# Six instead of eight experts with places of their own in a routed expert stage

## The chip, the cores and the metric

The kernel runs on one core of a Trainium2 chip, in one launch. The metric is device time in microseconds, the median over several executions. A profile of one further execution gives the engines' instructions (PE is TensorE, DVE VectorE, ACT ScalarE, POOL GpSimd, SP SyncE) and the packets of the DMA engines. All data are float32.

## The reference

One layer of a perceiver block on 256 tokens of width 512: attention to 4096 context tokens and to the tokens themselves, then a state-space mixer, then a mixture of experts. The change concerns only the last part. With x the normalized tokens:

```python
scores = sigmoid(x @ gate_w)                       # 256 x 32 experts
topk_w, topk_i = top_k(scores, 6)
topk_w = topk_w / (sum(topk_w) + 1e-20)
combine = sum(one_hot(topk_i, 32) * topk_w)        # 256 x 32
g = einsum('td,edf->tef', x, wg); u = einsum('td,edf->tef', x, wu)    # 192 wide for each expert
routed = einsum('tef,efd,te->td', silu(g) * u, wd, combine)
shared = (silu(x @ sg) * (x @ su)) @ sd
out = x_before + routed + shared
```

Every token uses 6 of 32 experts, so 1536 pairs of token and expert are computed rather than 8192. How many tokens an expert gets depends on the data. Counted with the reference on the inputs that it sets up, experts 0 to 7 get 19, 65, 18, 38, 100, 75, 55 and 21; the ten largest of the rest get 63 to 103, and the other fourteen 1 to 43.

## The kernel before

The kernel is one program written by hand in its order; a scheduler then settles how the instructions of each engine follow one another, and adds the waits. Attention and the mixer fill the span to about 800 us; the routing follows to 838 us, and the expert rounds from there to the end.

**Routing.** route(t) (lines 1003 to 1023) computes the gate for 128 tokens and picks six experts each. scatter(t) (1025) writes each token's row, six times, into a DRAM buffer xg, in which every expert has 256 rows. places() (1041) counts the tokens of every expert and ranks those experts that have no place of their own by their count; place_rows() (1099) turns the ranking into row numbers, one column of the table `place` for each transfer that has to find its expert through the table.

**Places.** The 32 experts are handled at 32 places, two at a time, in 16 rounds of a pair each. The first FIXED places belong to the experts of those numbers. The next ten are wide and go to the largest of the remaining experts. All places up to WIDE hold up to 128 tokens; the others are narrow and hold 64, so that both experts of a narrow pair share one tile of 128 tokens. If an expert has more tokens than its place, a flag (`crowded`, 1128) sends the program into a second arm (1574 to 1597), which redoes all pairs for two tiles of tokens each.

```python
FIXED = 8                                              # 57
WIDE = FIXED + 10                                      # 58
NPL = 2 * (NE - FIXED) + (NE - WIDE) // 2 - (NE - WIDE) + (NE - FIXED) // 2   # 62: columns of place
ZROW = WIDE * P + (NE - WIDE - TAIL) * HALFP           # 63: rows of the result buffer ye
```

**Weights.** A pair's weights are two pieces of 1 MB (gate, up and the first 128 rows of the down matrix, 8 KB for each of 128 partitions) and one of 256 KB (the rest of the down matrix). There are NHELD = 6 sets of buffers. load_weights (1173) loads a pair:

```python
if fixed:                                              # 1175
    for i in range(2):
        wait_for(nc.sync.dma_start(to[i], a["experts"][2 * n + i]), behind)
    nc.sync.dma_start(to[2], a["down_rest"][2 * n:2 * n + 2].rearrange("e p n -> (e p) n"))
else:
    s = 2 * n - FIXED                                  # 1180
    for i in range(2):
        rows_at(to[i], a["experts"].rearrange("e p n -> (e p) n"), s + i)
    rows_at(to[2], a["down_rest"].rearrange("e p n -> (e p) n"), NE - FIXED + s // 2)
```

A pair of fixed places is known beforehand: SP loads it by plain DMA (L1177, L1178) from hold() (1191), as soon as the mixer has finished with two large buffers. The others are found through the table: POOL issues an indirect DMA for each piece (rows_at, L1165) once place_rows has written the table: pairs 4 and 5 in the loop at 1306, and pair n + 5 in round n (load_pair, 1552), behind the down product that frees its buffers.

**Rounds.** The loop at 1524 runs over the pairs n. A wide round does gate_up (1430: two products of 128 tokens, written by project at L218, with silu on ACT and a product on DVE), fetches the tokens of pair n + 2 (fetch, 1353: SP and plain DMA, L1359, for a pair of fixed places, POOL and an indirect DMA otherwise), transposes the tokens of pair n + 1 (turn, L1369), computes the down product of pair n - 1 (down, L1458 and L1461) with two copies by ACT and two result writes to ye, and transposes its own hidden values (L1448). A narrow round has one token tile for both experts: gate_up_halves (L1388) runs two products on halves of the array, down_halves (L1410, L1411) gives one result tile and one write. The token tiles live in a ring of four buffers. The pairs 0 and 1 take their tokens by a product with a selection matrix (L1474) instead, and the last four pairs add their results on chip by another one (spread, L1428), rather than through ye. At the end POOL gathers the results of the other pairs from ye for each token (L1321), DVE adds them (L1329), and SP stores the output.

Of the kernel before, what the change touches and what calls it, by code (L numbers as in the profile page):

```python
# [53 lines left out]
WGU = KD * 2 * FE  # L54
WEX = WGU + DM
NHELD = 6
FIXED = 8
WIDE = FIXED + 10
HALFP = P // 2
HEAD = 4  # L60
TAIL = 8
NPL = 2 * (NE - FIXED) + (NE - WIDE) // 2 - (NE - WIDE) + (NE - FIXED) // 2
ZROW = WIDE * P + (NE - WIDE - TAIL) * HALFP
# [10 lines left out]
def perceiver_layer(ctx: ExitStack, tc: tile.TileContext, a: dict, out: bass.AP):  # L74
# [65 lines left out]
    def layer(ctx, bounded):  # L140
# [848 lines left out]
        def routing_memory():  # L989
# [8 lines left out]
            G.iota(m["p"], pattern=[[0, 1]], base=0, channel_multiplier=1, allow_small_or_imprecise_dtypes=True)  # L998
            V.tensor_scalar(m["free"], m["p"], float(FIXED), None, ALU.is_ge)

# [40 lines left out]
        def places():  # L1041


            mask, first, pos, key, keys, at, less = (m[n] for n in ("mask", "first", "pos", "key", "keys", "at", "less"))
            few, n, low = slice(0, NE), NE - FIXED, slice(FIXED, NE)

# [21 lines left out]

            wide = float(WIDE - FIXED)
            V.tensor_scalar(first[:, low], at[:, low], float(P), float(FIXED * P), ALU.mult, ALU.add)  # L1070
            V.tensor_scalar(less[:, low], at[:, low], wide, 0.0, ALU.subtract, ALU.max)
# [580 lines left out]
```

## Time and profile before

| | |
|---|---|
| median of 3 executions | 985.41 us (983.65 to 986.29) |
| the profiled execution | 989.13 us |
| its span, from first to last instruction | 987.4 us |
| granted TensorE clock | 0.998 |
| PE busy | 964.3 us, 98% |
| DVE, ACT, POOL busy | 496.5, 388.1, 205.0 us |
| moved by DMA | 125.65 MB, 41.16 MB of it on the software queue (POOL's) |

A line of instructions in the profile gives the source line, the engine, the operation and "out<-in" by the names of the tiles. A tile that reuses the memory of an older one carries the older one's name: the weight pieces appear as w_in, wkv, ctx, w_out, oacc, kT and lacc, the last piece as v or oacc. The releaser in brackets is what the profile infers to have ended an idle time. Times inside the span count from its start.

### The profile page before, as it was taken

To read this page: it belongs to the slowest core of one execution; us is meant where nothing else is said; L and a number is where in the kernel's file an instruction comes from. 1 tells how busy PE (TensorE), PEld (TensorE's weight loads), DVE (VectorE), ACT (ScalarE), POOL (GpSimd) and SP (SyncE) were. 2 spreads that over 40 slices of the span, in tenths; PEclk is the share of its full clock that TensorE was granted. 3 is DMA by queue.
4 is the path that set the end of the run, shared out by engine and by line. 5 is a ranking of instruction groups with operands and counts; after the bars stand their busy time and mean duration, and the time that the engine had idled before them with its cause. 6 is when DMAs were issued, how large, how long until landed. Compare 5 with 4: busy or idle time off the path is not lost.

```text
span 987.4 us, 8877 instructions
## 1 busy us (share of the span) xinstructions
PE 964.3 (98%) x2730; PEld 453.8 (46%) x2730; DVE 496.5 (50%) x1000; ACT 388.1 (39%) x854; POOL 205.0 (21%) x212
## 2 busy tenths in 40 slices
PE   7999999999999999999999999999999999999995
PEld 3444444444444444444444444444465655455442
DVE  3456554454454544544545445458587666521133
ACT  3645443443444434434434344344153731122220
POOL 4443001101100200200200110000013234545442
PEclk9999999999999999999999999999999999999999
DMA  9733232213304304304113121250046452899973
GB/s 317 237 74 98 76 95 91 71 32 117 85 11 139 85 1 149 75 11 150 53 33 97 67 51 32 72 152 1 0 150 206 171 188 111 319 342 352 381 292 107
DMA packets 131436, 125.65 MB, mean 127 GB/s; under 512 B 80209, under 2 KB 99570, under 8 KB 126130
## 3 DMA queue, kind: packets, MB, share of 16 engines
q1 hardware_dynamic: 119216, 77.96, 26.1%
q0 software_dynamic: 7984, 41.16, 11.4%
q10 hardware_dynamic: 4178, 5.85, 1.6%
q8 instruction: 24, 0.39, 0.2%
q14 instruction: 34, 0.28, 0.1%
HBM read 89.02 MB, written 35.93 MB: 127 GB/s over the span
## 4 chain that ended last, share of the span: by engine, by line
PE 94%; DVE 2%; ACT 1%; POOL 1%; issue 1%; DMA 1%; SPq 0%; DVEq 0%; ACTq 0%
PE oT L592 23%; PE scT L567 23%; PE ps_kv L364 17%; PE ps_egu L218 5%; PE ps_self L218 3%; PE ps_v L218 2%; PE ps_o L790 2%; PE ps_egu L1388 2%; PE ps_k L218 2%; PE ps_ye L1458 2%; PE ps_xbc L218 1%; PE ps_out L984 1%; PE ps_sgu L218 1%; PE xgTp L1369 1%; PE ps_ye L1461 1%; PE ps_yd L924 1%
## 5 line engine op out<-in xcount | busy, mean ns | idle before, releaser
L583 DVE TENSOR_TENSOR lacc<-lacc,prT 128x512 f32<-128x512 f32 x256 | 182.8, 715 | 238.9 <-ACT prT L573 238.2
L573 ACT ACTIVATE prT<-scT,bq,rk 128x512 f32<-128x512 f32 x256 | 198.9, 777 | 253.8 <-PE scT L567 241.7
L567 PE MATMUL scT<-qT,kT 128*128 128x512 f32 x536 | 271.6, 592 | 0.0
L592 PE MATMUL oT<-prT,v 128*128 128x512 f32 x528 | 268.3, 592 | 0.0
L567 PEld LDWEIGHTS scT<-qT,kT 128*128 128x128 f32 x536 | 101.1, 190 | 124.7 <-issue 122.4
L592 PEld LDWEIGHTS oT<-prT,v 128*128 128x128 f32 x528 | 100.2, 190 | 125.8 <-issue 115.5
L196 POOL TENSOR_TENSOR rk<-pv,mhalf 128x4 f32<-128x4 f32 x32 | 32.3, 1010 | 369.2 <-DVE pv L195 369.2
L364 PE MATMUL ps_kv<-wkv,fast 128*128 128x512 f32 x112 | 53.4, 592 | 0.0
L254 ACT ACTIVATE sq<-kraw 128x128 f32<-128x128 f32 x128 | 35.6, 278 | 45.3 <-DVE kraw L382 43.2
L364 PE MATMUL ps_kv<-wkv,ctx 128*128 128x512 f32 x112 | 52.8, 592 | 0.0
L364 PE MATMUL ps_kv<-fast,fast 128*128 128x512 f32 x112 | 52.6, 592 | 0.0
L598 DVE TENSOR_TENSOR oacc<-oT,oacc 128x512 f32<-128x512 f32 x64 | 43.7, 683 | 0.0
L364 PEld LDWEIGHTS ps_kv<-wkv,fast 128*128 128x128 f32 x112 | 21.3, 190 | 26.8 <-issue 26.8
L364 PEld LDWEIGHTS ps_kv<-fast,fast 128*128 128x128 f32 x112 | 21.3, 190 | 26.8 <-issue 21.8
L364 PEld LDWEIGHTS ps_kv<-wkv,ctx 128*128 128x128 f32 x112 | 21.3, 190 | 26.8 <-issue 23.7
L358 POOL TENSOR_TENSOR fast<-ctx 128x512 f32<-128x512 f32 x7 | 9.3, 1335 | 113.0 <-PE ps_kv L364 94.2
L382 DVE TENSOR_TENSOR kraw<-ps_kv,fast 128x256 f32<-128x256 f32 x42 | 17.9, 426 | 28.1 <-PE ps_kv L364 28.1
L1441 DVE TENSOR_TENSOR hid<-si,ps_egu 128x128 f32<-128x128 f32 x18 | 5.2, 287 | 51.7 <-ACT si L1439 49.0
L790 PE MATMUL ps_o<-wo,qT 128*128 128x512 f32 x64 | 28.8, 592 | 0.0
L218 PE MATMUL ps_self<-wq,xT 128*128 128x512 f32 x64 | 28.1, 592 | 0.0
L603 DVE RECIPROCAL lacc<-ps_l 128x512 f32<-128x512 f32 x8 | 26.8, 3349 | 0.1
L364 PE MATMUL ps_kv<-fast,ctx 128*128 128x512 f32 x56 | 26.3, 592 | 0.0
(379 smaller groups left out, 1120.8 us busy)
## 6 DMA issues: line engine op xcount, KB each, us to landing
xg<-xn SPq DMA_DIRECT2D x6, 2560.0 KB
ctx<-in_ctxT_dram SPq DMA_DIRECT2D x7, 1024.0 KB, 5.3
kd<-tr SPq DMA_DIRECT2D x112, 64.0 KB, 2.7
kT<-kd SPq DMA_DIRECT2D x28, 256.0 KB, 3.7
ye<-y_sb ACTq DMA_DIRECT2D x21, 256.0 KB, 7.9
wq<-in_wq_dram SPq DMA_DIRECT2D x4, 1024.0 KB
wo<-in_wo_dram SPq DMA_DIRECT2D x4, 1024.0 KB
w_in<-in_W_inT_dram SPq DMA_DIRECT2D x4, 1024.0 KB
```

The costliest lines, as they stand in the source:

```text
L196: return G.tensor_tensor(dst, v[:, :n], mhalf[:, :n], ALU.pow)
L218: TE.matmul(ps, lhs(k), rhs_of(k), start=(k == 0), stop=(k == KD - 1))
L254: S.activation(sq[:, h, :], raw[:, h, :], AF.Square, accum_out=ss[:, h:h + 1])
L364: TE.matmul(ps, lhs(k), rhs(k), start=(start and k == 0), stop=(k == 1), skip_group_check=True)
L567: scored.append(TE.matmul(sc, kT[:, g, i * P:(i + 1) * P], qT[:, t, heads4(g), :].rearrange("p h q -> p (h q)"), start=True, stop=True).ins)
L573: S.activation(pr, sc, AF.Exp, bias=shift, scale=SCALE if r is None else r[:, i, g:g + 1])
L583: V.tensor_tensor(la, la, pr, ALU.add)
L592: TE.matmul(outs[g, t], v[:, i, g * HD:(g + 1) * HD], pr, start=(n == 0), stop=last)
L598: V.tensor_tensor(ov, outs.pop((g, t)), ov, ALU.add)
L603: V.reciprocal(rl, ps)
L790: TE.matmul(m["ps_o", t], aT[:, t, h, :], wo[j][:, h % 4, :], start=(h == 0), stop=(h == NH - 1))
L1388: TE.matmul(ps[self.half(i)], xT[:, k, self.half(i)], w[i][:, k, :], start=(k == 0), stop=(k == KD - 1))
```

## The change

Two places fewer are fixed. As WIDE is FIXED + 10, ten wide places remain for the experts that are ranked, now 26 of them, and sixteen places instead of fourteen are narrow. Pairs 0 to 2 are fixed, 3 to 7 wide and found through the table, 8 to 15 narrow; before it was 0 to 3, 4 to 8 and 9 to 15. The table `place` has 57 columns instead of 53. With the counts above, experts 6 and 7 come to narrow places, and the same ten experts as before to the wide ones.

```diff
 NHELD = 6
-FIXED = 8
+FIXED = 6
 WIDE = FIXED + 10
 HALFP = P // 2
```

## The prediction

> **What bounds the kernel now.** I read the profile's head and its chain first: whose time is the span made of?
>
> ```profile
> span 987.4 us, 8877 instructions
> ...
> PE 94%; DVE 2%; ACT 1%; POOL 1%; issue 1%; DMA 1%; SPq 0%; DVEq 0%; ACTq 0%
> ```
>
> TensorE is the chain almost throughout, so a round of it that becomes shorter is worth its full difference, until something else ends last. The diff only bears on the expert rounds, from about 838 us on, and on what feeds them. The chain in order of time, there (start, length, group), gives the period of a round:
>
> ```profile
> 909.77 5.16 PE ps_egu L218 x16
> ...
> 919.06 5.16 PE ps_egu L218 x16
> ...
> 927.91 2.73 PE ps_egu L1388 x16
> ...
> 934.38 2.73 PE ps_egu L1388 x16
> ...
> 939.98 2.73 PE ps_egu L1388 x16
> ```
>
> L218 is the gate/up product of a wide pair, L1388 that of a narrow one. A wide round takes 919.06 - 909.77 = 9.29 us; the last wide one 8.85 (it turns a single token tile for its successor); the first narrow one 6.47 (it still has a wide pair's down product); a narrow one after that 5.60.
>
> Then the stage in windows of 10 us (length; busy time and count of PE, weight loads, DVE, ACT, POOL; granted clock, DMA share, GB/s):
>
> ```profile
> 840.00:850.00 10.00, 10.00 (x28) 4.88 (x27) 8.51 (x32) 1.17 (x2) 7.56 (x9) 1.00 0.69 237
> 850.00:860.00 10.00, 8.34 (x27) 4.26 (x27) 4.04 (x19) 1.80 (x5) 1.59 (x2) 1.00 1.01 409
> 860.00:870.00 10.00, 9.93 (x43) 5.73 (x39) 3.32 (x8) 2.32 (x5) 5.25 (x7) 1.00 0.96 338
> 870.00:880.00 10.00, 10.00 (x40) 5.43 (x39) 2.12 (x6) 2.22 (x5) 5.23 (x6) 1.00 0.90 316
> ...
> 920.00:930.00 10.00, 10.00 (x43) 4.96 (x43) 1.44 (x5) 2.83 (x7) 5.09 (x6) 1.00 1.00 375
> 930.00:940.00 10.00, 10.00 (x48) 3.93 (x46) 2.65 (x8) 2.31 (x6) 3.76 (x4) 1.00 1.02 399
> 940.00:950.00 10.00, 10.00 (x53) 4.01 (x54) 2.54 (x8) 2.28 (x6) 3.78 (x4) 1.00 1.01 417
> 950.00:960.00 10.00, 10.00 (x52) 4.16 (x52) 1.52 (x6) 2.38 (x6) 3.78 (x4) 1.00 0.50 164
> ```
>
> PE is full and at full clock, but so are the 16 DMA engines, from 850 to 950. They fall idle only some 13 us before the last round starts (964.03). The DMA stands just behind PE, and this change adds to it.
>
> Last, POOL's instructions and the transposes of token tiles (L1369) in order of time:
>
> ```profile
> 843.21 1.15 POOL L1165 DMA_INDIRECT w_out<-in_experts_dram,place  x1 [0.31 <-issue]
> ...
> 859.14 0.94 POOL L1165 DMA_INDIRECT w_in<-in_experts_dram,place  x1 [8.41 <-DMA xg_sb<-xg]
> ...
> 924.93 0.95 POOL L1165 DMA_INDIRECT xg_sb<-xg,place  x1 [3.33 <-PE xgTp L1369]
> ...
> 942.71 0.95 POOL L1165 DMA_INDIRECT xg_sb<-xg,place  x1 [0.30 <-issue]
> ```
>
> ```profile
> 867.43 1.04 PE L1369 MATMUL xgTp<-ident,xg_sb 128*128 128x128 f32 x8
> ```
>
> 843.21 is the first load of pair 4, 859.14 the first of pair 6, 924.93 the token tile of pair 13, 942.71 that of pair 14. The trace's packets on the software queue move in the order in which POOL issued them: pair 4 from 845.1 to 852.8, pair 5 to 860.1, pair 6 to 868.7, and only then the tokens fetched behind it (868.4 to 872.9). At the end, pair 15's weights end at 950.7, and the tiles of pairs 14 and 15 land at 951.6 and 952.9. The tile of pair 14 is transposed at 953.84: little to spare.
>
> **The change, part by part.** FIXED goes from 8 to 6 and WIDE, being FIXED + 10, from 18 to 16.
>
> *One wide round becomes narrow.* Wide pairs are 0 to 7, not 0 to 8. From the periods: 9.29 - 5.60 = **3.69 us less PE**. With nothing late, the gate products start at 909.77 + 8.85 = 918.62 (pair 8), then 925.09, 930.69, 936.29, 941.89 (pair 12); pair 15's is 3.69 earlier.
>
> *Bytes that go.* One token tile and one result write (256 KB each), and a wide round's second set of ACT and DVE steps, all beside PE.
>
> *Pair 3's weights move from SP to POOL.* Before, three SP DMAs loaded them ahead of the rounds, by 818 us; no PE wait there names them. So they leave idle time and enter the full stretch: 2 x 1.05 + 0.26 = 2.36 MB. Its two token tiles move from SP (L1359) to POOL too. In the built kernel POOL's order is: pairs 3, 4, 5, the two tiles of pair 3, pair 6, the tiles of pair 4, pair 7, and so on. Five more issues cost POOL 5 x 1.25 = 6.3 us, inside the 8.41 us it idled before 859.14: pair 6's load is not issued later. Nothing is left behind on SP. Each POOL DMA also waits for the landing of the eighth one before it; the tiles of pair 3, ninth and tenth after pair 3's first load, wait for loads that land by 854, about when POOL reaches them.
>
> *First place where this can bite: pair 3's tiles.* By 861.0, 5.77 MB had moved (pairs 4 and 5, four token tiles on SP). The changed queue needs 3 x 2.36 + 4 x 0.26 = 8.12 MB for pairs 3 to 5 and the tiles of pairs 2 and 3: 2.35 MB more, at 400 GB/s (the mean of the windows with a share of 1.00 or more: 409, 375, 399, 417) 5.9 us, so 866.9. From a last packet to its reader I take 1.3 us (the last result packet at 953.9, the gather that needs it at 955.27). Ready at 868.2 against 867.43: PE stands for 0.8 us. Bounds: 0 and, at the 364 GB/s found below, 1.4. Later tiles also come behind one weight pair more (the tiles of pair 6 behind pair 8's weights, where before they preceded them), with some 2 to 4 us left of the 12.2 before (landed at 884.0, turned at 896.18).
>
> *Second place: pair 13's tile.* Before, POOL fetched it ahead of pair 13's weights; in the built kernel it comes behind pair 15's, in one group with pairs 14 and 15. PE meets that partly: it puts the down product of pair 11 (1.97 us), a hidden transpose (0.31) and the first part of pair 12's down product (0.48) ahead of the turn. So without lateness the turn would start at 941.89 + 2.73 + 1.97 + 0.31 + 0.48 = 947.4.
> When does the tile land? Before: 12 pairs (28.3 MB), 20 token tiles and 20 result writes (10.5 MB) moved from 845.1 until pair 14's tile at 951.6: 38.8 MB in 106.5 us, 364 GB/s. After, up to pair 13's tile: 13 pairs (30.7), 18 token tiles and 19 result writes (9.7): 40.4 MB. Full engines at 400 GB/s would take 101.0 us (946.1); the old mean of 364, 111 us (956.1). Before, 106.5 - 38.8 / 400 = 9.5 us went into gaps and slow starts. The start stays (1.49 MB in the 4.9 us to 850: 1.2 us lost), as do waits for a buffer PE has yet to free; but with one pair more in the queue it runs dry less often (shares of 0.90 to 0.96 before). I keep 5.5 us, between the ends of 0 and 9.5: landing 845.1 + 101.0 + 5.5 = 951.6, ready at 952.9. **PE stands 5.5 us.**
>
> The early 0.8 us is not added: it moves the turn from 947.4 to 948.2 and shortens the second stall by as much, since transfers set the end there. Everything behind the turn (gate products of 13 and 14, the final sums) follows PE as before; the last gathers need the down product of pair 11, which now precedes the stall.
>
> *A page that speaks against the change.* The trace first: windows with full engines move 375 to 417 GB/s. The Trainium skill, "DMA: Bandwidth & Descriptors", section "Bandwidth", holds that between HBM and SBUF the HBM side binds at about 358 GB/s per core, under the fabric's 435. An estimate from that page: 40.4 MB take 112.8 us, the tile is ready at 959.2, PE stands 11.8 us, and the kernel loses 8.1. The trace stays above 358 for 30 us on end (920 to 950), so I take the trace; the mean of 364 keeps the page's case alive.
>
> *Small ones.* The placing steps on DVE work on 26 columns for 24 (0.17 to 0.23 us each, set by no such width): nothing.
>
> **Sum.** -3.7 + 5.5 = **+1.8 us**, on a profiled run of 989.13 us with a span of 987.4: 989.2 span. The median of the runs shown is 985.41, 3.7 below the profiled run; the difference carries over: **987.2 us**.
>
> **The rivals.** All three turn on the mean rate R from 845.1 to pair 13's landing; my case is R = 379. No change would need 386.
> - *Transfers keep up.* From R = 397 up, the tile is ready before 948.2 and at least 2.9 us of the 3.7 stay: down to **981.7**. For it: 399 and 417 GB/s in 930 to 950. Against it: no stretch of 50 us held that.
> - *The old mean was the ceiling, slower.* At 364 GB/s the tile is ready at 957.4, PE stands 10.0 us: **991.7**. It decides from 375 down, where the stall passes 3.7 + 3.0. For it: 870 to 920 ran at 316 to 367 with shares of 0.90 to 0.98, so little of it was empty time. Against it: POOL's issues of pairs 7 to 12 waited for PE.
> - *The small places overflow.* Were one of the moved experts over 64 tokens, the second arm would redo all pairs, 32 wide rounds of 9.29 us: +297. By the reference's own choice on these inputs, experts 6 and 7 get 55 and 21 tokens; I give it nothing.
>
> **How the numbers follow.** 0.3% (3.0 us) is about what a measurement of this kernel can tell from no change. My case, R from 376 to 390, has a chance of 0.53 and its own range of 984.3 to 988.2: all of it the same. Transfers that keep up: 0.09, of which 0.07 faster by over 0.3%. The old mean: 0.38, slower. Together 0.07, 0.55, 0.38. The range reaches from 983.0, which leaves out most of the faster case, to 992.0, a little over the old mean's time.
>
> **What would show it.** In the profile after: wide rounds 9.3 and narrow rounds 5.6 us apart, 8 of L1388 rather than 7; PE idle ahead of the turn of pair 13's tile (L1369) by 4 to 6 us, at 947 to 953; a first, small wait at 867; DMA share near 1.00 from 850 to 952. I am wrong if that turn doesn't wait (the gain then stands), if wide rounds stretch well over 9.3 us from 870 on (tokens late in each), or if the POOL order on the chip isn't that of the build.

## The result and the profile after

| | kernel before | changed kernel |
|---|---|---|
| median | 985.07 us (983.44 to 986.30, 9 executions) | 989.54 us (986.87 to 991.13, 9 executions) |
| ratio | | 1.0046 (95%: 1.0037 to 1.0055) |
| profiled execution, and its span | 989.13 us, 987.4 us | 990.8 us, 989.1 us |

The changed kernel is 4.5 us slower: inside the forecast range, 2.3 us above the forecast, and slower by more than the 0.3% that counts as a difference here. The two profiled executions stand only 1.7 us apart, because the one of the kernel before lies 4 us above its median. Therefore stages are compared below, not whole profiles.

The chain in order of time, changed kernel (start, length, group), answers the five lines shown of before:

```profile
854.10 12.89 DMA xg_sb<-xg,place
...
883.60 5.16 PE ps_egu L218 x16
...
892.89 5.16 PE ps_egu L218 x16
...
911.47 5.16 PE ps_egu L218 x16
...
920.33 2.73 PE ps_egu L1388 x16
...
926.80 2.73 PE ps_egu L1388 x16
...
932.40 2.73 PE ps_egu L1388 x16
...
940.73 11.08 DMA xg_sb<-xg,place
```

The periods are those of before: 9.29 us (892.89 - 883.60), 8.86 for the last wide round, 6.47, 5.60. New are the first and the last line: the chain runs twice through the transfer of a token tile, which it didn't touch in the kernel before.

The windows of 10 us (length; busy time and count of PE, weight loads, DVE, ACT, POOL; granted clock, DMA share, GB/s):

```profile
850.00:860.00 10.00, 9.93 (x39) 5.31 (x38) 3.41 (x14) 2.38 (x6) 6.03 (x8) 1.00 1.01 414
860.00:870.00 10.00, 7.75 (x26) 4.52 (x25) 2.30 (x7) 1.14 (x3) 3.48 (x4) 0.90 1.02 419
870.00:880.00 10.00, 10.00 (x36) 5.28 (x35) 1.41 (x5) 2.21 (x5) 4.73 (x5) 0.93 1.00 393
...
940.00:950.00 10.00, 9.27 (x44) 3.38 (x40) 1.96 (x7) 2.38 (x6) 3.27 (x4) 1.00 1.01 416
950.00:960.00 10.00, 8.38 (x33) 3.01 (x33) 1.37 (x2) 0.90 (x2) 4.13 (x5) 0.83 0.45 145
```

PE loses time in two places, 860 to 870 and 940 to 960, and in or right behind both the granted clock is below 1.00 (0.90 and 0.93, then 0.83). TensorE's instructions in order of time name the cause (in brackets the idle time before the instruction, and what ended it):

```profile
867.12 1.70 PE L1369 MATMUL xgTp<-ident,xg_sb 128*128 128x128 f32 x8 [2.14 <-DMA xg_sb<-xg,place]
...
949.20 1.07 PE L1410 MATMUL ps_ye<-w_in,hidT 128*64 128x512 f32 x2 [0.73 <-ACT hidT L1403]
951.86 1.34 PE L1369 MATMUL xgTp<-ident,xg_sb 128*128 128x128 f32 x8 [1.59 <-DMA xg_sb<-xg,place]
```

The two lines of L1369 are the turns of pairs 3 and 13, the two places that the prediction named; the line between them is the first part of pair 12's down product. What follows the first wait is seen in windows of 1 us:

```profile
867.00:868.00 1.00, 0.77 (x5) 0.59 (x6) 0.21 (x1) 0.00 (x0) 0.00 (x0) 1.00 0.99 414
868.00:869.00 1.00, 1.00 (x5) 0.95 (x5) 0.62 (x2) 0.00 (x0) 0.00 (x0) 0.51 1.01 426
869.00:870.00 1.00, 1.00 (x2) 0.34 (x1) 0.55 (x1) 0.00 (x0) 0.00 (x0) 0.50 1.04 434
870.00:871.00 1.00, 1.00 (x2) 0.34 (x1) 0.00 (x0) 0.00 (x0) 0.20 (x1) 0.50 0.99 418
871.00:872.00 1.00, 1.00 (x4) 0.17 (x4) 0.00 (x0) 0.00 (x0) 0.75 (x1) 0.79 0.98 401
```

After a stand of 2.1 us, TensorE lost 0.49 + 0.50 + 0.50 + 0.21 = 1.7 us more to the clock, almost as much as to the wait itself. Behind the second wait the clock is 0.67, 0.50, 0.50 and 0.62 in the windows from 953 to 957, which is 1.7 us again.

### The profile page after: what moved, and what is told of

Its sections match the earlier page's. It is cut to its first block, busy times and chain, and to the rows that moved or that the text cites. A ratio compares the mean times of both kernels' runs of the same rounds, so it can differ in the third digit from the quotient of the medians.

```text
span 989.1 us, 8840 instructions
## 1 busy us (share of the span) xinstructions
PE 964.4 (98%) x2723; PEld 452.1 (46%) x2723; DVE 496.7 (50%) x998; ACT 387.1 (39%) x852; POOL 208.1 (21%) x216
## 4 chain that ended last, share of the span: by engine, by line
PE 90%; DMA 4%; POOL 2%; DVE 1%; ACT 1%; issue 1%; SPq 0%; DVEq 0%; POOLq 0%
PE scT L567 23%; PE oT L592 23%; PE ps_kv L364 17%; PE ps_self L218 3%; PE ps_egu L218 3%; DMA xg_sb<-xg,place 2%; PE ps_v L218 2%; PE ps_o L790 2%; PE ps_egu L1388 2%; PE ps_k L218 1%; PE ps_xbc L218 1%; PE ps_out L984 1%; PE ps_ye L1458 1%; PE ps_sgu L218 1%; PE xgTp L1369 1%
## 5 line engine op out<-in xcount | busy, mean ns | idle before, releaser
L218 PE MATMUL ps_self<-wq,xT 128*128 128x512 f32 x64 | 28.1, 592 | 0.0
```

The source lines that it names most:

```text
L218: TE.matmul(ps, lhs(k), rhs_of(k), start=(k == 0), stop=(k == KD - 1))
```

## The experiments

**Theory A**, after the first comparison: the waits for token tiles and the slow clock behind them are the change's whole cost. **Theory B**: the transfer engines are simply full, and no order of the transfers helps. Both had to give way to a third one, C, below.

The experiments ran on other chips than the first comparison. There the kernel before has medians of 989.3, 989.6, 991.0 and 990.2 us (group by group), so each ratio is to the kernel before in the same group. A ratio weighs all executions and can differ from that of the medians by up to 0.1%. For the profiles I cut the rounds in three: from the first product of round 0 to the first product of pair 4 ("start"), from there to the first product of pair 15 ("middle"), and from there to the end of the span ("tail"). All readings are starts of L218, L1388 and the span.

| kernel | start | middle | tail | ratio |
|---|---|---|---|---|
| before, first profile | 36.7 | 82.30 | 23.4 | |
| changed, first profile | 39.1 | 84.45 | 21.2 | 1.0046 |
| before again | 36.1 | 82.30 | 26.0 | |
| changed again | 45.8 | 82.91 | 20.8 | 1.0063 |
| pair 3 moved, nothing narrower | 40.4 | 82.30 | 25.9 | 1.0069 |
| one round narrower, nothing moved | 36.5 | 85.57 | 20.6 | 0.9976 |
| pair 3's tiles first | 44.6 | 82.51 | 21.0 | 1.0053 |
| pair 13's tile first | 45.8 | 78.60 | 25.3 | 1.0042 |
| both first | 45.1 | 78.61 | 26.2 | 1.0047 |
| pair 13's tile first, with a filler | 46.5 | 78.61 | 25.2 | 1.0065 |
| before, with five small issues more | 45.9 | 82.30 | 26.5 | 1.0080 |
| paced, both tiles first | 36.1 | 78.81 | 25.6 | 0.9963 |
| paced, pair 13's tile behind | 36.3 | 82.59 | 21.0 | 0.9978 |
| paced, both behind | 39.1 | 85.71 | 21.1 | 0.9997 |

### First group: the token tiles first

Pair 3's token tiles issued directly behind pair 3's own weights:

```diff
-        for n in range(FIXED // 2, NHELD):
-            load_pair(n)
+        load_pair(FIXED // 2)
         actx.close()
...
             yp = rctx.enter_context(tc.tile_pool(name="yp", bufs=6))
+            main.fetch(2)
+            main.fetch(3)
+            for n in range(FIXED // 2 + 1, NHELD):
+                load_pair(n)
...
-            fetched = set()
+            fetched = {2, 3}
```

> The changed kernel, with the two token tiles of pair 3 issued on POOL right behind pair 3's weights, ahead of those of pairs 4 and 5. Theory A (the loss is two waits of PE for token tiles that stand behind weights in POOL's queue, 2.3 us at pair 3's and about 2.3 at pair 13's, each followed by some 3.6 us at half clock that cost 1.8 more): the first wait and its slow clock vanish (4.1 us), but PE then comes earlier to the second wait, which transfers set, so only 1 to 3 us come back: 986.5 to 988.5. Theory B (the DMA engines are simply full, in any order the same bytes come at the same time): as the changed kernel, 989.5, within 1 us.

Measured: 1.0053 (1.0033 to 1.0074), 994.4 us.

The narrow pairs' token tiles issued one round earlier, so that pair 13's stands ahead of the weights of the pairs 14 and 15:

```diff
-                for f in range(n + 2, n + 4 if n == LAST else n + 3):
+                for f in range(n + 2, n + 5 if 2 * n >= WIDE else n + 3):
```

> The changed kernel, with the token tiles of narrow pairs fetched up to two rounds earlier, so that POOL issues pair 13's ahead of the weights of pair 14 and pair 14's ahead of those of pair 15; the first wait stays. Theory A: the second wait and the slow clock behind it vanish, 4 to 6 us: 983.5 to 985.5. Theory B: 989.5, within 1 us, with PE waiting for weights or for pair 15's tile instead.

Measured: 1.0042 (1.0031 to 1.0053), 994.0 us.

Both edits together:

> Both reorderings together. Theory A: no wait for tokens is left, and the whole 3.7 us of the narrower round stay: 981.4 (980.5 to 982.5), clock at 0.998. Theory B: 987 to 989.5.

Measured: 1.0047 (1.0031 to 1.0063), 993.9 us.

The second kernel with two matrix products that nothing reads, put ahead of the turn of pair 3 to keep TensorE busy there:

```diff
                     src = self.rows.pop((n, i))
+                    if i == 0 and n in FILL:
+                        for _ in range(FILL[n]):
+                            TE.matmul(tp.rearrange("p k n -> p (k n)"), ident, xn[:, 0, :], start=True, stop=True)
```

> e2_tokens13_first with two products of 128x512 that nobody reads (1.7 us) on PE just ahead of the transposes of pair 3's tokens, so that PE waits there for about 0.6 us rather than 2.3 before the same tile. The output is the reference's. Theory A: the granted clock no longer halves behind that wait, and the 1.8 us of slow running are saved: 1.8 us under e2_tokens13_first. Rival (the slow clock is not set off by PE's standing still): the clock halves all the same, time within 0.5 us of e2_tokens13_first, or the products only add to it.

Measured: 1.0065 (1.0045 to 1.0084), 996.2 us. There was no wait at the turn of pair 3 left to fill in that profile, so it tests nothing; the two products only add work.

What follows: the edits did what they were to do. With pair 13's tile first the middle takes 78.60 us, 3.70 less than the kernel before, and no turn waits. Still the time is no better. Theory A misses by up to 8 us, even when the 4.2 us are taken off by which the kernel before is slower on this chip. Theory B comes near the ratios, but it has the wrong place: the loss is in the start, before any token tile is late. The profile of "both first" has one wait of TensorE that neither profile of the first comparison had at that length, 7.5 us ahead of the hidden transpose L1447 (L1448 in the changed kernel), at 858 us.

### Second group: the two halves of the change

**Theory C**, from these profiles: ACT's silu of the first round starts 8 to 9 us after the product that it needs has left TensorE, and it starts 1.6 to 2.4 us after the last instruction in POOL's row of load issues. POOL's issues, or what they set off, hold TensorE's count back; moving pair 3 to POOL lengthens that row.

The kernel before again:

> The kernel before itself, one profile on the chip of this group. Theory A (the waits for token tiles, and the slow clock behind them, are the whole of the change's cost): the first two rounds run as in its first profile, with at most 2 to 3 us of TensorE standing for hid between 845 and 860 us. Theory C (while POOL issues its loads one behind the other onto full transfer engines, TensorE's count for the first round's products reaches ScalarE late, until about 2 us after the last of these issues): the last of the six issues ends near 851 us, so TensorE stands for hid until 852 to 853 us, 2 to 4 us in all.

Measured: 990.35 us, one execution.

The changed kernel again:

> The changed kernel itself, with a second profile. Theory A: 1.0046 of the kernel before as on the first chip; the profile shows two waits for token tiles of 2 to 4 us (turns of pairs 3 and 13), each with some 3.4 us of half clock behind it, and nothing over 1 us between 845 and 860 us. Theory C: eleven POOL issues end near 856 us, so TensorE stands for hid until 857 to 859 us, 6 to 8 us in all; buffers come free as much later, and the waits for token tiles shrink below 2 us.

Measured: 1.0063 (1.0050 to 1.0077), 996.3 us. TensorE in order of time, changed kernel again:

```profile
844.62 5.32 PE L218 MATMUL ps_egu<-w_in,xc 128*128 128x384 f32 x16
...
859.64 0.69 PE L1448 MATMUL hidTp<-ident,hid 128*128 128x128 f32 x2 [8.09 <-DVE hid L1441]
```

ACT and POOL of the same execution:

```profile
849.11 0.33 ACT L1439 ACTIVATE si<-ps_egu 128x192 f32<-128x192 f32 x1 [3.70 <-remote]
858.94 0.33 ACT L1439 ACTIVATE si<-ps_egu 128x192 f32<-128x192 f32 x1 [9.50 <-remote]
```

```profile
842.79 1.15 POOL L1165 DMA_INDIRECT wkv<-in_experts_dram,place  x1 [0.30 <-issue]
...
855.63 0.95 POOL L1165 DMA_INDIRECT xg_sb<-xg,place  x1 [0.30 <-issue]
```

The sixteen products of round 0 end at 849.94. The second silu needs only these and starts at 858.94, 9.0 us later; DVE's product and TensorE's transpose follow it. The trace also records when each engine raises its count. TensorE's count for the sixteen products rises at 858.91, and the one for the four products behind them, which ended at 851.55, at 858.99. Four products take 1.5 us, so if the products themselves had been late, the two counts could not stand 0.08 us apart. The count was late, not the work.

POOL issued without a break until 856.58: a row of seventeen, six writes of token rows (L1028) from 834.90 on and these eleven loads. In the kernel before again the row has twelve (six and six) and ends at 849.93, and the second silu starts at 851.57. POOL's last issue of the row, then ACT, there:

```profile
848.98 0.95 POOL L1165 DMA_INDIRECT oacc<-in_down_rest_dram,place  x1 [0.30 <-issue]
```

```profile
851.57 0.33 ACT L1439 ACTIVATE si<-ps_egu 128x192 f32<-128x192 f32 x1 [2.54 <-PE ps_egu L218]
```

The windows of the changed kernel again, and then those of the kernel before again:

```profile
850.00:860.00 10.00, 1.91 (x7) 1.03 (x8) 2.83 (x13) 0.33 (x1) 5.05 (x6) 0.75 1.02 417
860.00:870.00 10.00, 10.00 (x27) 5.05 (x26) 0.84 (x4) 1.62 (x4) 1.85 (x2) 0.74 0.60 229
```

```profile
850.00:860.00 10.00, 8.87 (x32) 4.52 (x31) 3.19 (x15) 2.05 (x5) 1.87 (x2) 1.00 1.04 408
860.00:870.00 10.00, 9.93 (x41) 5.56 (x40) 3.33 (x8) 1.85 (x5) 5.33 (x6) 1.00 0.96 361
```

Both have full transfer engines between 850 and 860 (shares of 1.02 and 1.04). TensorE is busy for 1.91 us in the one and 8.87 in the other, and the mean clock is 0.75 in the one and 1.00 in the other. Full engines alone don't make the difference.

Pair 3 moved, but eighteen wide places as before:

```diff
-WIDE = FIXED + 10
+WIDE = FIXED + 12
```

> Pair 3 at wide places of its own on POOL's queue, but eighteen wide places as before: no round is narrower, so 3.7 us of products stay and the transfers are those of the kernel before. Theory A: one wait for pair 3's token tiles, 2.3 us with 1.8 us of slow clock, and none at pair 13: 1.004 of the kernel before (+4 us). Theory C: 5 to 8 us of standing for hid in the first two rounds and its slow clock: 1.006 to 1.010.

Measured: 1.0069 (1.0049 to 1.0090), 997.0 us. Here the second silu came early (852.97), but the copy of the hidden values behind it stood until 860.05, 2.4 us after POOL's last issue.

The kernel before with one round narrower and nothing moved:

```diff
-WIDE = FIXED + 10
+WIDE = FIXED + 8
...
-            V.tensor_scalar(crowded, m["key"][0:1], float(P), None, ALU.is_gt)
+            V.tensor_scalar(crowded, m["key"][0:1], float(2 * P), None, ALU.is_gt)
```

> Eight experts with places of their own and pair 3 on SP as before, but eight chosen wide places instead of ten: one round narrower and nothing moved. It leaves out what expert 25's two tokens beyond 64 should add to the result (the second pass for crowded places is switched off for it). Both theories: 3.7 us less of products, so 0.9963 of the kernel before, unless the shorter rounds make the last wide pairs wait for their tiles. Theory A: any such wait is at the turns of pairs 11 to 14, below 3 us. Theory C: standing for hid in the first two rounds of 2 to 4 us, as in the kernel before, until about 2 us after the sixth issue.

Measured: 0.9976 (0.9968 to 0.9984), 987.2 us. TensorE in order of time, at the turn of pair 13:

```profile
951.12 0.66 PE L1369 MATMUL xgTp<-ident,xg_sb 128*128 128x128 f32 x4 [2.50 <-DMA xg_sb<-xg,place]
```

So the narrower round is a gain of 2.4 us by itself, though the wait for pair 13's tile comes with it; the move alone costs 6.8 us (both by the ratios). Their sum, 4.4 us, is 1.8 short of the changed kernel's 6.2 in this group, with intervals of about 1 us on each side. On these chips the move is the loss.

### Third group: what in the move

**Theory D**, the rival of C: the full transfer engines hold TensorE's count back, whoever issues.

Five POOL issues more behind pair 5's weights in the kernel before, of 8 KB each, so five issues as in the move and next to no bytes:

```diff
             yp = rctx.enter_context(tc.tile_pool(name="yp", bufs=6))
+            extra = rctx.enter_context(tc.tile_pool(name="extra", bufs=1))
+            for i in range(5):
+                rows_at(extra.tile([P, 16], FP, tag=f"x{i}", name="extra"),
+                        xg.rearrange("r (c e) -> (r c) e", e=16), NE - FIXED)
```

> The kernel before, with five more POOL issues directly behind pair 5's weights; each gathers 8 KB into a tile that nothing reads, so the bytes stay the same to 0.1 per cent. They use the same eight completion lanes, so the third to fifth may wait for pair 4's weights (853 to 856 us). Theory C (the issues themselves hold TensorE's count back until 1.6 to 2.4 us after the last of an unbroken row): the count for the first round's second product comes at 854.5 us or later instead of 851.5 to 852.6 us, and the time grows by 3 to 8 us (1.003 to 1.008). Theory D (full transfer engines hold it back, whoever issues): it comes by 853 us as in the kernel before, and the time is 1.000 to 1.002.

Measured: 1.0080 (1.0061 to 1.0099), 999.3 us. POOL and then ACT in this profile:

```profile
848.51 0.95 POOL L1165 DMA_INDIRECT oacc<-in_down_rest_dram,place  x1 [0.31 <-issue]
849.77 0.95 POOL L1165 DMA_INDIRECT extra<-xg,place  x1 [0.30 <-issue]
...
854.76 0.94 POOL L1165 DMA_INDIRECT extra<-xg,place  x1 [0.30 <-issue]
```

```profile
858.27 0.33 ACT L1439 ACTIVATE si<-ps_egu 128x192 f32<-128x192 f32 x1 [8.17 <-remote]
```

The row now ends at 855.70, and the silu starts 2.6 us after it, at 858.27; in the kernel before again it was 851.57. Five issues that move nothing to speak of cost 8.4 us (7.9 by the ratio). Theory D expected at most 1.002.

The changed kernel with the row cut to six loads: pairs 3 and 4, then pair 3's token tiles and pair 5's weights only once the first round's hidden values are there. Pair 13's tile is issued early as in the first group.

```diff
-        for n in range(FIXED // 2, NHELD):
+        for n in range(FIXED // 2, NHELD - 1):
             load_pair(n)
...
-            G.indirect_dma_start(out=out, out_offset=None, in_=src,
+            dma = G.indirect_dma_start(out=out, out_offset=None, in_=src,
...
+            if not_before:
+                tc.add_manual_dep(dma.ins, not_before.pop().name, mybir.DependencyInfo(
+                    mybir.DependencyClass.Sync, mybir.DependencyReason.DATA), reason="paced")
...
-            fetched = set()
+            fetched = {3}
...
                 (main.gate_up if wide else main.gate_up_halves)(n)
+                if n == 0:
+                    not_before.append(main.done[0])
+                    main.fetch(3)
+                    load_pair(NHELD - 1)
...
-                for f in range(n + 2, n + 4 if n == LAST else n + 3):
+                for f in range(n + 2, n + 5 if 2 * n >= WIDE else n + 3):
```

> The changed kernel with POOL's first row of issues cut to six: weights of pairs 3 and 4, as long as the row in the kernel before; pair 3's token tiles and then pair 5's weights wait for the first round's hid, and the token tiles of the narrow pairs stand before the weights of the next pair. Theory C: TensorE's count comes near 852 us as in the kernel before, the waits for token tiles are gone too, and the 3.7 us of products are seen: 0.9955 to 0.9975 of the kernel before; if the five issues behind hid hold the counts a second time, TensorE stands again near 855 to 860 us and it is 1.002 or more. Theory D: the engines are as full as in the changed kernel, so it stands as long as there, until 857 to 859 us, and the time is 1.003 to 1.006.

Measured: **0.9963 (0.9950 to 0.9977), 987.0 us against 991.0**: faster than both kernels, and with the whole of the work. POOL, then ACT, in the paced kernel:

```profile
848.93 0.95 POOL L1165 DMA_INDIRECT oacc<-in_down_rest_dram,place  x1 [0.31 <-issue]
852.62 0.95 POOL L1165 DMA_INDIRECT xg_sb<-xg,place  x1 [2.74 <-DVE xc L1509]
```

```profile
851.57 0.33 ACT L1442 ACTIVATE si<-ps_egu 128x192 f32<-128x192 f32 x1 [3.92 <-PE ps_egu L218]
```

The row ends at 849.88 and the silu starts 1.7 us later, as early as in the kernel before. The start takes 36.1 us as there, and the 3.7 us of products come out at the end.

From the row's end to the second silu's start it is 1.6 to 1.9 us in the eight profiles where the row ends with weights (before twice, narrow only, pair 3's tiles first, both first, the three paced ones), 2.4 in the three where it ends with token tiles (changed again, pair 13's tile first, the filler), and 2.6 with the small issues. The first profile of the changed kernel is the exception: its row of seventeen ended at 856.30, and the second silu started at 849.74, 0.05 us after the products' end. In that execution each of TensorE's 151 counts from 838 us on rises within 0.03 us of the end of its products. Why nothing was held there isn't known. (The fourteenth profile is that of pair 3 moved with nothing narrower, above.)

### Fourth group: the token tiles, with the hold out of the way

The paced kernel with both token tiles behind the weights, as in the changed kernel (the order of fetch and load_pair in round 0 swapped, the fetch range as in the change):

```diff
-                    main.fetch(3)
                     load_pair(NHELD - 1)
+                    main.fetch(3)
...
-                for f in range(n + 2, n + 5 if 2 * n >= WIDE else n + 3):
+                for f in range(n + 2, n + 4 if n == LAST else n + 3):
```

> The changed kernel with POOL's first row cut to six as in the paced kernel (0.9963), but pair 3's token tiles stand behind pair 5's weights and pair 13's behind pair 15's, as in the changed kernel. Theory A: with the long hold gone, both waits for token tiles show: 2 to 4 us at the turn of pair 3 with up to 3.4 us of half clock behind it, and 3 to 5 us at the turn of pair 13 with the same: 1.001 to 1.005. Theory B (the transfers keep up with these rounds, and the hold was all of it): no wait above 1 us, 0.996 to 0.998.

Measured: 0.9997 (0.9988 to 1.0006), 989.9 us. This is the changed kernel with its row cut and nothing else changed, so it is the cleanest test of the row: 0.9997 where the changed kernel again has 1.0063, or 6.5 us for one break. POOL's last issue of the row, then ACT:

```profile
848.33 0.95 POOL L1165 DMA_INDIRECT oacc<-in_down_rest_dram,place  x1 [0.30 <-issue]
```

```profile
851.18 0.33 ACT L1442 ACTIVATE si<-ps_egu 128x192 f32<-128x192 f32 x1 [2.54 <-PE ps_egu L218]
```

The paced kernel with pair 13's tile alone behind (the second hunk only):

> As the paced kernel, with pair 3's token tiles first, but pair 13's token tile behind pair 15's weights as in the changed kernel: the second place alone. Theory A: TensorE stands 3 to 5 us at the turn of pair 13, with up to 3.4 us of half clock behind it: 0.999 to 1.003. Theory B: no wait above 1 us there, 0.996 to 0.998.

Measured: 0.9978 (0.9967 to 0.9990), 987.1 us.

Neither theory has it whole; Theory B's range holds the second time, but both turns wait over 1 us. The turn of pair 13 waits in both (1.8 and 1.4 us named, 6.9 and 3.8 us more in the middle than the paced kernel). But with pair 13's tile alone behind, the time grows by 1.5 us only, with an interval that reaches zero: the tail of its profile is 4.6 us shorter. The reason is seen in the tail of the paced kernel, TensorE in order of time:

```profile
969.71 2.08 PE L1431 MATMUL total<-y_sb,xc 128*128 128x512 f32 x2 [3.51 <-ACT y_sb L1426]
```

There POOL issues eleven of the twelve gathers of results (L1321 in the kernel before) in one row from 951.84 to 965.86, and TensorE stands again, for 3.5 us, with half clock behind it (0.50 from 970 to 975). It is the same hold: work of TensorE that ended from 963.86 on has its counts raised only between 969.01 and 969.18, five in a burst, 3.2 us after the row's end. Where pair 13's tile is late, eight gathers end at 960.92, the others wait for DVE, the held counts follow from 962.61 on, and TensorE doesn't stand. POOL in the paced kernel, then with pair 13's tile behind:

```profile
964.91 0.95 POOL L1324 DMA_INDIRECT yk<-ye,row_y  x1 [0.30 <-issue]
```

```profile
959.98 0.95 POOL L1324 DMA_INDIRECT yk<-ye,row_y  x1 [0.30 <-issue]
962.93 1.34 POOL L1324 DMA_INDIRECT yk<-ye,row_y  x1 [2.01 <-DVE x_sb L1332]
```

So the late tile pays part of its price back by breaking a row of issues. This is read from the profiles; no run broke that row by itself.

The 1.9 us between these two kernels can't be put to pair 3's tiles. In the kernel with both behind, the turn of pair 3 doesn't wait; the scheduler has put pair 1's down product ahead of the turn of pair 2 there, and TensorE stands 1.6 us for the copy of its hidden values. That run compares two orders, not two transfers; and the two profiles lie 1.5 us above and below their medians.

## Why the prediction held, and where it failed

**One round narrower, 3.7 us: right.** The middle is 82.30 us in four profiles with eighteen wide places and 78.60 to 78.81 in four with sixteen and no late tile.

**POOL's five more issues at nothing: wrong, and the largest error.** They did fit into the 8.41 us in which POOL idled, and pair 6's load was not what suffered. But the cover named was POOL's own time. The cost lay elsewhere: a longer unbroken row of issues holds the first round up. On the chips of the experiments this is +9.7 us in the start (45.8 against 36.1), of which 7.0 are TensorE's stand in the window 850 to 860, and most of the rest is the slow clock. In the first comparison's profile of the changed kernel the hold is absent, so there it explains nothing.

**First place, 0.8 us: right place, wrong size.** On the first chip the turn of pair 3 waited 2.1 us, and the clock took 1.7 more. The tile was not slower than forecast: it was ready at 867.1, where 868.2 was expected. TensorE was early. It had finished at 864.98 (862.24 + 2.74), not at 867.43. The profile of before has two short stands for the hidden values in the first round, 0.85 and 0.81 us, a small hold of the same kind:

```profile
851.21 0.30 PE L1448 MATMUL hidTp<-ident,hid 128*128 128x128 f32 x1 [0.85 <-DVE hid L1442]
...
853.67 0.46 PE L1448 MATMUL hidTp<-ident,hid 128*128 128x128 f32 x2 [0.81 <-DVE hid L1441]
```

The profile of the changed kernel has neither, and its first round starts 0.7 us sooner (844.37 against 845.03). The bounds, 0 to 1.4, varied the transfer rate alone and took TensorE's time as it stood in one profile. The granted clock stood in every window that the prediction showed, but it wasn't asked what a wait does to it.

**Second place, 5.5 us: the tile's time right, the cost right by luck, the sum wrong.** The tile was ready at 951.9 (forecast 952.9): 40.4 MB over 951.9 - 1.3 - 845.1 us, 383 GB/s against 379. But TensorE came to the turn at 950.3 (949.20 + 1.07), not at 947.4, so it stood 1.6 us, not the 4 to 6 that were to show it. It was late by 1.7 us from the first place (pair 4's products began at 883.44, before at 881.73), by 0.7 us of waiting for ACT's copy of pair 12's hidden values, and by 0.6 us because the first part of pair 12's down product took 1.07 us and not 0.48.

Still the middle took 84.45 us instead of 78.6, 5.8 more: 2.3 us of waits, 1.7 of slow clock and some 1.8 in neither. Of these last, 1.1 us is in that down product. Its two halves run side by side when the turn comes first, and one behind the other when the turn comes between them. TensorE in the kernel before again, at an earlier narrow pair, and then in the changed kernel again at the turn of pair 13, where the clock stayed at 1.00 (and the middle took 82.91):

```profile
941.25 0.66 PE L1369 MATMUL xgTp<-ident,xg_sb 128*128 128x128 f32 x4
941.83 1.08 PE L1410 MATMUL ps_ye<-w_out,hidT 128*64 128x512 f32 x4
```

```profile
956.19 1.07 PE L1410 MATMUL ps_ye<-w_in,hidT 128*64 128x512 f32 x2 [0.73 <-ACT hidT L1403]
958.98 1.33 PE L1369 MATMUL xgTp<-ident,xg_sb 128*128 128x128 f32 x8 [1.72 <-DMA xg_sb<-xg,place]
960.24 1.07 PE L1410 MATMUL ps_ye<-w_in,hidT 128*64 128x512 f32 x2
```

The sum also counted a stall here in full at the end, and the tail returned 2.2 us against the profile of before, 4.5 to 5.4 us in the later groups.

By the table, the two profiles of the first comparison differ by +2.4 us in the start, +2.1 in the middle (-3.7 and +5.8) and -2.2 in the tail, +2.4 us in all; the medians differ by +4.5. Most of what is left is that the profile of before lies 4.1 us above its median and that of the changed kernel 1.3. The small hold may be part of these 4.1 us; no profile of the kernel before without it is on record. The forecast of +1.8 was near because a first wait too small and a second one with no return partly cancelled, and its range held because it reached to the old mean rate.

**The page on bandwidth** ("DMA: Bandwidth & Descriptors", section "Bandwidth"), which would have given +8.1: the trace was the better guide. The paced kernel, windows of 10 us:

```profile
850.00:860.00 10.00, 8.64 (x31) 4.33 (x30) 2.05 (x10) 2.05 (x5) 5.67 (x6) 1.00 1.02 411
860.00:870.00 10.00, 9.94 (x41) 5.56 (x40) 3.23 (x8) 1.74 (x6) 5.27 (x6) 1.00 1.03 421
870.00:880.00 10.00, 10.00 (x44) 5.83 (x42) 2.36 (x7) 2.68 (x6) 5.13 (x7) 1.00 1.02 413
880.00:890.00 10.00, 10.00 (x42) 5.70 (x41) 3.09 (x8) 2.31 (x5) 4.72 (x5) 1.00 1.04 407
```

Forty microseconds at 407 to 421 GB/s are no queue limited to 358. The same section's other figure, 425 GB/s measured with one core alone for 16 MB, is nearer.

**The rivals.** Transfers that keep up: no, pair 13's tile was late wherever it stood behind the weights. The old mean as a ceiling (991.7): no, 383. Crowded places: no second arm ran. The rival that counted was not among them: the issues themselves.

**What stays open.** Which part of the chip holds the count is not shown. What is shown is that five issues without bytes bring a long hold, that a break in the row shortens it to that of the kernel before (stands of 1.1 to 1.4 us in the three paced profiles, 1.1 in the kernel before again), and that the counts are late while the products aren't. A later row of ten issues in the paced kernel (852.62 to 864.81) held nothing that TensorE waited for, so the length alone is not the rule. Only one execution of the changed kernel on the first chip was profiled, and how many of the others had a hold isn't known; so the split of the 4.5 us there rests on that one. Breaking the row of gathers in the tail as well was not tried; by the table (25.6 against 21.0) it might be worth some 4 us, an estimate.

## What to carry to other kernels

Ask of every moved transfer not only when its data land and whether the issuing engine has time, but how long the unbroken row of issues becomes and which other engine's first result falls into it; here one wait cut the row of POOL issues, and the kernel lost nothing by it. Where PE may wait some 2 us, count a half clock behind it as well, 1.7 us here. Don't take a start time from one profile as fixed: a stand in it may be gone in the next. And before adding a stall to a sum, look at what the next stage was waiting for: here the tail took much of it back.

## What the runs showed of the hardware

- A row of some twelve to seventeen POOL DMA issues, 1.25 us each, delayed TensorE's count, and with it ACT's first look at a finished product, by up to 9.0 us, until 1.6 to 2.6 us after the row's end, in 13 of 14 profiles. Five issues of 8 KB were worth 8.4 us of kernel time. With the row cut and the transfer engines as full (share 1.02 in the paced kernel), TensorE stood for 1.4 us.
- TensorE fell to half clock after a stand of 2.1 us, for about 3.4 us, and after stands of 7 to 8 us for longer (clock 0.75 and 0.74 over 850 to 870). Stands of 1.6 us (first profile) and 1.7 us (changed kernel again) at the turn of pair 13, each with one of 0.7 us shortly before it, differed: the first brought half clock, the second did not. The Trainium skill, "TensorE: Matmul & The Clock Gate", section "What's actually happening", lets the clock fall after an idle window of about 3.4 us; here less was enough.
- Products on the two halves of the array overlapped: four of the down product took 1.08 us side by side (L1410), and two of one half alone 1.07.
